# The adjacency transposed by VectorE inside the attention, with key tiles of every 13th node

## Chip, core and metric

The kernel runs on one NeuronCore of one Trainium2 chip. The metric is the device time of one execution in microseconds (us), as the median of the runs shown. One profiled execution stands beside them; its rows are used for durations. A core has five engines that run side by side: TensorE (PE; its weight loads are shown apart as PEld), VectorE (DVE), ScalarE (ACT), GpSimd (POOL) and SyncE (SP), which here issues most transfers. Sixteen DMA engines move the data between HBM and the on-chip memories.

## What is computed

Four graph layers on 3327 nodes with 128 features, each as `x = x + layer(relu(layernorm(x)))`. Only the first one is attention, and it takes most of the time. Its reshape makes 128 heads (`d`) of 8 elements (`h`) out of the projections, and the adjacency is added to the scores twice:

```python
def _L0_gnn_ref(x, spatial_encoding, edge_encoding, Wq, Wk, Wv, Wo):   # both encodings are adj
    n, d = x.shape
    h = Wq.shape[0] // d                       # 8
    scale = d ** (-0.5)
    q = (x @ Wq.T).reshape(d, n, h)
    k = (x @ Wk.T).reshape(d, n, h)
    v = (x @ Wv.T).reshape(d, n, h)
    a = jnp.einsum('dnh,dmh->dnm', q, k) * scale
    a = a + spatial_encoding + edge_encoding
    a = jax.nn.softmax(a, axis=2)
    out = jnp.einsum('dnm,dmh->dnh', a, v)
    out = out.reshape(n, h * d)
    return out @ Wo.T
```

Layers 1 and 2 are hyperbolic graph convolutions with one product `adj @ y` each. Layer 3 is a message layer with two, by rows and by columns of adj. All is in float32.

## The kernel before

The attention works on transposed scores: keys stand on the 128 partitions, queries along the free axis. So it needs adj transposed (keys by queries), and the three later layers read the same transposed copy, `adjT`, from HBM in strips.

**Head of the program.** Three stages stand ahead of the attention, each with its own pools.

- Stage a (L243 to L291): weights are transposed on TensorE, x is loaded and normalised, h is transposed (L213). Then a loop over 13 pairs of node tiles (L259) projects k, q and v (L268). q is split into a rounded half (`st_hi`, ACT, L278) and the rest (`st_lo`, DVE, L279); k is stored unsplit to `kraw_d`; squares of q and k (ACT, L281) are summed to squared norms (DVE, L283). `places` (L238) writes q and k by 1 KB runs.
- Stage b (L294 to L321): adj is read in 7 blocks of 512 rows (L302), the row maxima are taken (DVE, L305), 676 transposes on TensorE (L312) make `adjT`, where key tile tm holds the nodes tm, tm+26, tm+52 and so on: the weight operand of the transpose is `r[:m, i, tm:N:NT]`, a read with a step of 26 elements. ACT and DVE copy the results out (`evac`), SP and POOL store them (L321).
- Stage c (L328 to L377): k is read back, split into halves and reordered so that each key tile is contiguous, with reads of step 26 (L338 on ACT, L339 on DVE), and stored as `kS_d` (L341). Beside it a bound of each row's scores is worked out (norms of q and k, plus the row maximum of adj), which later stands in for the softmax's maximum, and one number, `wide`, which selects between a general path (L399, not taken with these inputs) and the fast one (L530).

**The attention** (L530 to L672) loops over 7 chunks of 476 queries, 32 groups of 4 heads and 13 pairs of key tiles: 2912 pairs. Its order is written out by hand (`manual_schedule`): one slot per head of a pair, `exps` in each slot, `scores` and `values` every second slot, `seed` and `loads` at fixed places of the four slots. For one pair u:

- `seed` (DVE, L573) copies two tiles of adj^T less the bound into two PSUM banks. Three sets of banks are used in turn, by u modulo 3.
- `scores` (PE, L579) adds the head's scores: a weight load of 64 partitions by 128 keys, `KT[b][64 * r:64 * r + 64, max(0, j - 1), q * P:(q + 1) * P]`, and 476 columns of q. Heads 1 to 3 add the difference to the head before, so a bank serves four heads in turn.
- `exps` (ACT, L591) takes exp of both banks, 952 columns. For two of three pairs the fourth head's is split in two, so that the first bank comes free earlier.
- `values` (PE, L599) multiplies by v, which stands in `VA` with a column of ones, into `po`; `store` (L611, L615) writes `po` out at the end of a group.
- `load_qk` (L488, L490, L492) brings the next group's k and q on SP's queue, `load_v` (L505) its v, `negate_q` and `spread_v` (POOL, L500, L510) prepare them, and `all_here` (POOL, L514) marks that all has come; the group's first score matmul waits for it. `load_adj` (L520, L521) brings the next chunk's adj^T.

The buffers of e stand in one ring of 16 (L464).

**After the attention** the output projection and three layers follow (L675 to L931), with `aggregate` (L747) reading strips of adjT or adj.

Of the kernel before, what the change touches and what calls it, by code (L numbers as in the profile page):

```python
# [10 lines left out]
F32 = mybir.dt.float32  # L11
# [11 lines left out]
P = 128  # L23
N = 3327
# [5 lines left out]
NQ = NT // 2  # L30
HEADS = D
# [25 lines left out]

def rows_of(t):
    return P - 1 if t == NT - 1 else P
# [15 lines left out]

@with_exitstack
def gnn_kernel(ctx: ExitStack, tc: tile.TileContext, x, adj, Wq, Wk, Wv, Wo, embed, layer,
# [8 lines left out]
    adjT = dram.tile([NT, P, NP], F32, name="adjT")  # L86
    v_d = dram.tile([NP, HD], F32, name="v_d")
    kraw_d = dram.tile([H, GP], F32, name="kraw_d")
# [3 lines left out]
    kS_d = dram.tile([2, H, HEADS, NP], F32, name="kS_d")  # L92
    oT_d = dram.tile([H + 1, GP], F32, name="oT_d")
    bound_d = dram.tile([NP], F32, name="bound_d")
    shift_d = dram.tile([HEADS, NP], F32, name="shift_d")

    rowmax = const.tile([P, NT], F32, name="rowmax")
    nc.vector.memset(rowmax, 0.0)
# [143 lines left out]

    with tc.tile_pool(name="a1", bufs=1) as a1, tc.tile_pool(name="a2", bufs=2) as a2, \  # L243
            tc.tile_pool(name="a_ps", bufs=4, space=PSUM) as a_ps:
        w_t = {"q": weight_T(a1, a_ps, Wq, "wq", "by element", HALF_SCALE),
               "k": weight_T(a1, a_ps, Wk, "wk", "by element"), "v": weight_T(a1, a_ps, Wv, "wv")}
        xs = load_x(a1)
# [9 lines left out]
        n2 = {s: a1.tile([P, NT, P], F32, name=f"n2{s}") for s in "qk"}  # L257
        v_rows = v_d.rearrange("(p t) d -> p t d", t=NT)
        for t0 in range(0, NT, 2):  # L259
            st = {s: a2.tile([P, H, 2 * P], F32 if s == "k" else F32R, name=f"st_{s}") for s in ("k", "hi", "lo")}  # L260
            sv = a2.tile([P, 2, HD], F32, name="st_v")
            for i in range(2):
                t = t0 + i
                for s in "kqv":
                    sq = a2.tile([P, HD], F32, name="sq")
                    for b in range(2):
                        ps = a_ps.tile([P, 512], F32, name="ps_m")
                        nc.tensor.matmul(ps, hT[:, t * P:(t + 1) * P], w_t[s][:, b * 512:(b + 1) * 512],  # L268
                                         start=True, stop=True)
                        if s == "v":  # L270
                            evac(sv[:, i, b * 512:(b + 1) * 512], ps)
                            continue
                        by_e = ps.rearrange("p (e i) -> p e i", e=4)
                        part = (slice(None), slice(4 * b, 4 * b + 4), slice(i * P, (i + 1) * P))
                        if s == "k":
                            evac(st["k"][part], by_e)
                        else:
                            nc.scalar.copy(st["hi"][part], by_e)  # L278
                            nc.vector.tensor_tensor(st["lo"][part], by_e, st["hi"][part].bitcast(F32),  # L279
                                                    op=ALU.subtract)  # L280
                        nc.scalar.activation(sq[:, b * 512:(b + 1) * 512], ps, AF.Square)  # L281
                    if s != "v":
                        nc.vector.tensor_reduce(n2[s][:, t, :], sq.rearrange("p (e i) -> p i e", e=H),  # L283
                                                axis=AX.X, op=ALU.add)
            nc.sync.dma_start(places(kraw_d, t0, 2, H), st["k"])
            for i, half in enumerate(("hi", "lo")):
                nc.sync.dma_start(places(qS_d, t0, 2, H, i * H * GP), st[half].bitcast(F32))
            nc.gpsimd.dma_start(v_rows[:, t0:t0 + 2], sv)
        for s in "qk":
            nc.gpsimd.dma_start(bass.AP(tensor=n2_d[s].tensor, offset=n2_d[s].offset,  # L290
                                        ap=[[NT * P, P], [1, NT * P]]), n2[s].rearrange("p t i -> p (t i)"))  # L291


    with tc.tile_pool(name="b_in", bufs=2) as b_in, tc.tile_pool(name="b_st", bufs=8) as b_st, \  # L294
            tc.tile_pool(name="b_ps", bufs=6, space=PSUM) as b_ps:
        for b in range(7):
            ts = tiles_of(b)
            nt = len(ts)
            r = b_in.tile([P, 4, N], F32, name="r")
            for i, t in enumerate(ts):  # L300
                for p0, p1 in pieces(rows_of(t)):
                    nc.sync.dma_start(r[p0:p1, i, :], adj[t * P + p0:t * P + p1, :])  # L302
            for i, t in enumerate(ts):
                m = rows_of(t)
                nc.vector.tensor_reduce(rowmax[:m, t:t + 1], r[:m, i, :], axis=AX.X, op=ALU.max)  # L305
            w = min(4 * P, N - b * 4 * P)
            for tm in range(NT):
                mp = rows_of(tm)
                ps = b_ps.tile([P, 4 * P], F32, name="ps_a")
                for i, t in enumerate(ts):  # L310
                    m = rows_of(t)
                    nc.tensor.transpose(ps[:mp, i * P:i * P + m], r[:m, i, tm:N:NT], ident[:m, :m])  # L312
                st = b_st.tile([P, 4 * P], F32, name="st_a")
                if mp < P:
                    nc.vector.memset(st, NOTHING)
                evac(st[:mp, :w], ps[:mp, :w])
                wp = w
                if b == 6:
                    nc.vector.memset(st[:mp, w:w + 1], 0.0)
                    wp += 1  # L320
                (nc.sync if tm % 2 else nc.gpsimd).dma_start(adjT[tm, :, b * 4 * P:b * 4 * P + wp], st[:, :wp])  # L321


    def head_rows(tensor):

        return bass.AP(tensor=tensor.tensor, offset=tensor.offset, ap=[[N, HEADS], [1, N]])

    with tc.tile_pool(name="c1", bufs=1) as c1, tc.tile_pool(name="c2", bufs=2) as c2, \  # L328
            tc.tile_pool(name="c_ps", bufs=2, space=PSUM) as c_ps:
        for e in range(H):  # L330
            raw = c2.tile([P, NP], F32, name="raw")
            nc.gpsimd.memset(raw[:, N:NP], 0.0)
            nc.sync.dma_start(raw[:, :N], head_rows(kraw_d[e]))
            by_tile = raw.rearrange("d (p q r) -> d r q p", q=NQ, r=2)
            hi = c2.tile([P, 2, NQ, P], F32R, name="hi")
            lo = c2.tile([P, 2, NQ, P], F32R, name="lo")
            for r in range(2):
                nc.scalar.copy(hi[:, r], by_tile[:, r])  # L338
                nc.vector.tensor_tensor(lo[:, r], by_tile[:, r], hi[:, r].bitcast(F32), op=ALU.subtract)  # L339
            for i, half in enumerate((hi, lo)):  # L340
                nc.gpsimd.dma_start(kS_d[i, e], half.bitcast(F32).rearrange("d r q p -> d (r q p)"))  # L341

        kn = c1.tile([P, NP], F32, name="kn")
        nc.sync.dma_start(kn[:, :N], head_rows(n2_d["k"]))
        km2 = c1.tile([P, 1], F32, name="km2")
        nc.vector.tensor_reduce(km2, kn[:, :N], axis=AX.X, op=ALU.max)
        qn = c1.tile([P, NP], F32, name="qn")
        nc.gpsimd.memset(qn[:, N:NP], 0.0)
        nc.sync.dma_start(qn[:, :N], head_rows(n2_d["q"]))
        nc.vector.tensor_scalar(qn, qn, km2[:, 0:1], 1e-30, op0=ALU.mult, op1=ALU.max)  # L350
        b2 = c1.tile([P, NT], F32, name="b2")
        for b in range(7):
            ts = tiles_of(b)
            ps = c_ps.tile([P, 4, P], F32, name="ps_b")
            for t in ts:
                nc.tensor.transpose(ps[:, t - 4 * b, :], qn[:, t * P:(t + 1) * P], ident)
            nc.vector.tensor_reduce(b2[:, ts[0]:ts[-1] + 1], ps[:, :len(ts), :], axis=AX.X, op=ALU.max)
        bmax = c1.tile([P, NT], F32, name="bmax")
        nc.scalar.activation(bmax, b2, AF.Sqrt)


        sh = c1.tile([P, NT], F32, name="sh")
        nc.vector.tensor_tensor(sh, bmax, rowmax, op=ALU.add)
        ps = c_ps.tile([P, P], F32, name="ps_k")
        nc.tensor.transpose(ps[:NT, :], sh, ident)
        shT = c1.tile([NT, P], F32, name="shT")
        nc.vector.tensor_copy(shT, ps[:NT, :])
        nc.sync.dma_start(bound_d.rearrange("(t p) -> t p", p=P), shT)

        fm = c1.tile([P, 1], F32, name="fm")  # L370
        nc.vector.tensor_reduce(fm, bmax, axis=AX.X, op=ALU.max)
        ps = c_ps.tile([P, P], F32, name="ps_k")
        nc.tensor.transpose(ps[:1, :], fm, ident)
        fm1 = c1.tile([1, 1], F32, name="fm1")
        nc.vector.tensor_reduce(fm1, ps[:1, :], axis=AX.X, op=ALU.max)
        wide = c1.tile([1, 1], I32, name="wide")
        nc.vector.tensor_scalar(wide, fm1, BOUND_MAX, None, op0=ALU.is_gt)  # L377
# [584 lines left out]
```

## Time and profile before

| | |
|---|---|
| median of 3 runs | 11876.81 us (11876.61 to 11879.45) |
| the profiled execution | 11879.07 us, span 11877.3 us |
| first exponential of the attention starts | 631.42 us |
| attention's last results copied out (L611) | 10761.22 us |
| ACT, L591, all exponentials | 10113.3 us busy, x13589 |
| PE, L599 and L579 | 5738.3 and 5089.5 us busy |
| DVE, L573, seeds | 3731.4 us busy, x5824 |

Times in a profile are us from the span's start unless marked ns. A group row holds line, engine, operation, result <- operands and count, then busy time and the mean of one in ns, then the engine's idle time just before those instructions and what ended it. Matmul ends are modelled, and records of one engine may overlap, so a busy share near 1 says that work follows work, not that the engine is at its peak.

### The profile page before, as it was taken

The numbers are of one execution on the slowest core, as the hardware profiler recorded it, in microseconds if no ns is written. First come the engines' busy times: TensorE is split into PE (matmuls) and PEld (weight loads), VectorE is DVE, ScalarE is ACT, GpSimd is POOL, SyncE is SP. The second block draws the span as 40 slices with busy tenths as digits, with TensorE's granted clock in tenths as the row PEclk, the third lists the DMA queues.
The fourth block names the chain that finished last, engine by engine and source line by source line (L and its number), as shares of the span: only waits on it lengthen the run. The fifth ranks groups of instructions, "written<-read, shape, count | busy, mean of one in ns | idle before, by whom it ended". The sixth has DMA issues, their size and how long they took to land.

```text
span 11877.3 us, 198965 instructions
## 1 busy us (share of the span) xinstructions
PE 11104.5 (93%) x73475; PEld 3593.7 (30%) x73475; DVE 4792.9 (40%) x7005; ACT 10457.3 (88%) x14062; POOL 1796.7 (15%) x3069
## 2 busy tenths in 40 slices
PE   6399999999999999999999999999999999996668
PEld 3322222222222222222222222222222222224334
DVE  7533333333333333333333333333333333335335
ACT  4389999999999999999999999999999999993100
POOL 0121111211121111211112111121111211110000
PEclk8699999999999999999999999999999999997789
DMA  8954444444454444544445444454444444442356
GB/s 293 367 107 79 78 82 98 84 76 82 78 101 81 77 83 76 105 77 80 80 78 104 76 84 76 81 101 79 81 76 83 99 82 79 78 85 91 137 192 239
DMA packets 532633, 1242.80 MB, mean 105 GB/s; under 512 B 148783, under 2 KB 405842, under 8 KB 509394
## 3 DMA queue, kind: packets, MB, share of 16 engines
q1 hardware_dynamic: 482013, 1051.27, 43.5%
q0 software_dynamic: 49648, 178.72, 4.6%
q8 instruction: 592, 9.70, 0.4%
q14 instruction: 380, 3.11, 0.1%
HBM read 1082.84 MB, written 146.55 MB: 104 GB/s over the span
## 4 chain that ended last, share of the span: by engine, by line
ACT 40%; PE 38%; DVE 11%; issue 9%; DMA 2%; POOL 0%; DVEq 0%; SPq 0%; POOLq 0%; ACTq 0%
ACT e L591 39%; PE S L579 16%; PE po L599 16%; DVE S L573 8%; PE pu L758 4%; PE ps_t L744 1%; PE ps_m L268 1%; DMA strip<-adjT 1%; DVE OS L611 0%; PE ps_y L703 0%; POOL adjT L321 0%; DVE s L193 0%; ACT tmp L191 0%; DMA adjT<-st_a 0%; DVE s L761 0%
## 5 line engine op out<-in xcount | busy, mean ns | idle before, releaser
L591 ACT ACTIVATE e<-S 128x952 f32<-128x952 f32 (+3 forms) x13589 | 10113.3, 915 | 14.2 <-PE S L579 7.7
L573 DVE COPY S<-a 128x476 f32<-128x476 f32 (+1 forms) x5824 | 3731.4, 655 | 6250.5 <-ACT e L591 5997.5
L599 PE MATMUL po<-e,VA 128*9 128x476 f32 (+1 forms) x46592 | 5738.3, 564 | 15.9 <-DVE OS L611 2.3
L579 PE MATMUL S<-QS,KT 64*128 64x476 f32 (+1 forms) x23296 | 5089.5, 443 | 112.9 <-DVE S L573 30.9
L579 PEld LDWEIGHTS S<-QS,KT 64*128 64x128 f32 x23296 | 2278.8, 184 | 5393.9 <-DVE S L573 2714.3
L615 POOL DMA_DIRECT2D oT_d<-OS x896 | 470.8, 531 | 6237.5 <-DVE OS L611 6157.0
L599 PEld LDWEIGHTS po<-e,VA 128*9 128x9 f32 x46592 | 691.3, 88 | 1790.4 <-issue 1691.0
L500 POOL TENSOR_SCALAR QS<-QS 32x476 fp32r<-32x476 f32 (+1 forms) x1344 | 781.9, 582 | 1034.5 <-DMA QS<-qS_d 537.7
L115 ACT COPY uT<-pu 128x494 f32<-128x494 f32 (+2 forms) x12 | 6.3, 528 | 459.2 <-PE pu L758 458.6
L758 PE MATMUL pu<-strip,y 128*128 128x494 f32 (+2 forms) x728 | 296.3, 570 | 92.8 <-DVE y L785 92.8
L758 PE MATMUL pu<-strip,h 128*128 128x494 f32 (+2 forms) x728 | 293.0, 564 | 68.9 <-DVE h L205 66.7
L510 POOL COPY VA<-VR 128x832 f32<-128x832 f32 x224 | 200.0, 893 | 962.8 <-DMA VR<-v_d 766.1
L312 PE MATMUL ps_a<-ident,r 128*128 128x128 f32 (+2 forms) x676 | 137.2, 374 | 129.2 <-DMA r<-in_adj_dram 65.3
L521 POOL TENSOR_TENSOR a<-a,shb 128x476 f32<-128x476 f32 (+1 forms) x182 | 213.1, 1203 | 239.7 <-DMA a<-adjT 239.6
L115 ACT COPY st_a<-ps_a 128x512 f32<-128x512 f32 (+3 forms) x91 | 48.5, 557 | 218.4 <-PE ps_a L312 98.1
L761 DVE TENSOR_REDUCE s<-strip 128x1 f32<-128x3327 f32 (+1 forms) x52 | 188.1, 3617 | 109.3 <-DMA strip<-adjT 63.0
L758 PEld LDWEIGHTS pu<-strip,y 128*128 128x128 f32 (+1 forms) x728 | 139.8, 192 | 248.7 <-issue 143.7
L758 PEld LDWEIGHTS pu<-strip,h 128*128 128x128 f32 (+1 forms) x728 | 138.4, 190 | 223.4 <-issue 140.7
L611 DVE COPY OS<-po 128x476 f32<-128x476 f32 (+1 forms) x224 | 145.6, 650 | 53.2 <-PE po L599 46.9
L312 PEld LDWEIGHTS ps_a<-ident,r 128*128 128x128 f32 (+2 forms) x676 | 115.8, 217 | 151.3 <-DVE st_a L119 53.5
L756 POOL DMA_DIRECT2D strip<-adjT x39 | 20.7, 532 | 793.6 <-PE pu L758 790.7
L213 PE MATMUL ps_t<-ident,h 128*128 128x128 f32 x78 | 20.3, 427 | 122.1 <-DVE h L205 108.1
(162 smaller groups left out, 1778.9 us busy)
## 6 DMA issues: line engine op xcount, KB each, us to landing
KT<-kS_d SPq DMA_DIRECT2D x1792, 208.0 KB
KT<-kS_d SPq DMA_DIRECT2D x1792, 104.0 KB
VR<-v_d SPq DMA_DIRECT2D x224, 416.0 KB
strip<-adjT POOLq DMA_DIRECT2D x39, 1663.5 KB, 8.5
strip<-adjT SPq DMA_DIRECT2D x36, 1663.5 KB
QS<-qS_d SPq DMA_DIRECT2D x3072, 14.9 KB
QS<-qS_d SPq DMA_DIRECT2D x1536, 29.8 KB
r<-in_adj_dram SPq DMA_DIRECT2D x25, 1663.5 KB
```

What stands on the lines that cost most here:

```text
L312: nc.tensor.transpose(ps[:mp, i * P:i * P + m], r[:m, i, tm:N:NT], ident[:m, :m])
L500: nc.gpsimd.tensor_scalar(QS[b][r0:r0 + 32, j + 1, :w], QS[b][r0:r0 + 32, j, :w].bitcast(F32), -1.0, 0.0, op0=ALU.mult, op1=ALU.add)
L510: nc.gpsimd.tensor_copy(VA[(c * NG + g) % 2][:, :, :, 0:H], v.rearrange("p j (t e) -> p t j e", e=H))
L521: nc.gpsimd.tensor_tensor(a[:, :w], a[:, :w], shift[:, :w], op=ALU.subtract)
L573: touch(u, [r], nc.vector.tensor_copy(bank(u, r), adj_of[c][2 * q + r][:, :w]))
L579: x = nc.tensor.matmul(bank(u, r), KT[b][64 * r:64 * r + 64, max(0, j - 1), q * P:(q + 1) * P], QS[b][64 * r:64 * r + 64, j, :w], start=Fa ...
L591: touch(u, range(a, b), nc.scalar.activation(e[:, a:b, :w], S[u % 3][:, lo + a:lo + b, :w], AF.Exp, scale=2.0))
L599: nc.tensor.matmul(po[32 * j:32 * j + H + 1, :w], VA[k % 2][:, 2 * q + r, j, :], e_of[u, j][:, at, :w], start=(q == 0 and r == 0), stop=(q ...
L611: nc.vector.tensor_copy(o[:, :w], po[:, :w])
L615: nc.gpsimd.dma_start(oT_d[:, d * N + c * CW:d * N + c * CW + w], o[32 * j:32 * j + H + 1, :w])
L758: nc.tensor.matmul(pu[c][:, :w], y[:m, t, :], s[:m, c * AW:c * AW + w], start=(t == 0), stop=(t == NT - 1))
L761: nc.vector.tensor_reduce(deg[:m, t:t + 1], s[:m], axis=AX.X, op=ALU.add)
```

## The change

- `adjT` is laid out by key in plain order (`[NP, NP]`). A key tile (r, q) holds every 13th node of one half of 1664 nodes, starting at q. So k can stay in the order of its projection: `kS_d` is written straight from stage a, split as q is, and `KT` is read by the score matmul with a step of 13 elements. The pass over `kraw_d` is gone.
- Stage b is gone. adj^T is made in 26 "squares" of 128 rows of adj, each as two halves of 1664 columns. A half is loaded so that each 32-row by 416-column part stands on a quarter of the partitions, is transposed by four DVE instructions in 32x32 blocks (`turn`), stored with runs of 512 bytes (`store`), and reduced to row maxima by four DVE instructions (`largest`). The row maxima go through HBM (`gather`, `back`) to the bound (`finish`).
- The first four squares, which the first chunk of queries needs, are made during stage a. The other 22 are made during the attention, at fixed pairs, in the chunk before the one that needs them: the load 4 pairs ahead of the first `turn`, then one DVE instruction per pair.
- Stage a projects q and k in one loop, and v in a second one. The sums of squares move from one DVE reduction to three POOL additions per tile. The bound is worked out in the middle of the v loop. x is loaded ahead of the weights.
- v of a group is loaded by two transfers with runs of 416 bytes in place of one with 832. The ring of 16 e buffers becomes one ring per head (5, 4, 3, 2). The general path is changed alike; it is not taken here.

```diff
-    adjT = dram.tile([NT, P, NP], F32, name="adjT")
+    adjT = dram.tile([NP, NP], F32, name="adjT")
+    by_key = adjT.rearrange("(r p q) n -> r q p n", r=2, q=NQ)
...
-    kS_d = dram.tile([2, H, HEADS, NP], F32, name="kS_d")
+    kS_d = dram.tile([2, H, GP], F32, name="kS_d")
...
+    class Square:
+        def load(self):
+            s, r = self.s, self.r
+            self.rows = self.pool.tile([P, 4, KW], F32, name="rows")
...
+            for i in range(4):
+                w = KW - (r == 1 and i == 3)
+                at = adj.offset + s * P * N + r * HALF + i * KW
+                nc.sync.dma_start(self.rows[32 * i:32 * i + 32, 0:whole, :w], bass.AP(
+                    tensor=adj.tensor, offset=at, ap=[[N, 32], [32 * N, whole], [1, w]]))
...
+            self.cols = self.pool.tile([P, NQ, P], F32, name="cols")
+        def turn(self, j):
+            nc.vector.transpose(self.cols[:, :, 32 * j:32 * j + 32],
+                                self.rows[:, j, :].rearrange("p (x q) -> p q x", q=NQ))
+        def store(self):
+            nc.sync.dma_start(by_key[self.r].rearrange("q p n -> p q n")[:, :, self.s * P:(self.s + 1) * P],
+                              self.cols)
+        def largest(self, rm, j):
+            nc.vector.tensor_reduce(rm[:, self.r, j:j + 1], self.rows[:, j, :], axis=AX.X, op=ALU.max)
...
+        for t0 in range(0, NT, 2):
+            for s, to in (("q", qS_d), ("k", kS_d)):
...
+                        nc.scalar.copy(st[0][part], by_e)
+                        nc.vector.tensor_tensor(st[1][part], by_e, st[0][part].bitcast(F32), op=ALU.subtract)
+                        nc.scalar.activation(sq[:, 4 * b:4 * b + 4, :], by_e, AF.Square)
+                    for m in (4, 2, 1):
+                        nc.gpsimd.tensor_tensor(n2[:, i:i + 1, :] if m == 1 else sq[:, 0:m, :],
+                                                sq[:, 0:m, :], sq[:, m:2 * m, :], op=ALU.add)
+                for half in range(2):
+                    nc.sync.dma_start(places(to, t0, 2, H, half * H * GP), st[half].bitcast(F32))
...
+            if t0 % 6 == 0 and len(bounds) < squares_of(0):
+                bounds.append(squares(a_t, len(bounds), a1))
+                bounds[-1].gather()
...
+            if t0 == 12:
+                wide = bound_scores()
...
-            v = e2.tile([P, 4, NT * H], F32, name="VR", bufs=1)
-            nc.sync.dma_start(v, bass.AP(tensor=v_d.tensor, offset=v_d.offset + 4 * g * N * H,
-                                         ap=[[NT * H, P], [N * H, 4], [1, NT * H]]))
+            for r in range(2):
+                nc.sync.dma_start(v[:, :, r * NQ * H:(r + 1) * NQ * H], bass.AP(
+                    tensor=v_d.tensor, offset=v_d.offset + (4 * g * N + r * HALF) * H,
+                    ap=[[NQ * H, P], [N * H, 4], [1, NQ * H]]))
...
-                        bank(u, r), KT[b][64 * r:64 * r + 64, max(0, j - 1), q * P:(q + 1) * P],
+                        bank(u, r), KT[b][64 * r:64 * r + 64, max(0, j - 1), q::NQ],
...
-                e = e_of[u, j] = e_e.tile([P, 2, CW], F32, name="e")
+                e = e_of[u, j] = e_e.tile([P, 2, CW], F32, name=f"e{j}", bufs=(5, 4, 3, 2)[j])
...
+            def plan_squares(c):
+                for k, s in enumerate(range(squares_of(c), squares_of(c + 1))):
+                    b = Bound(e_t, s)
+                    for r in range(2):
+                        sq, u = Square(e_t, s, r), (c * NG + 6 * k + 3 * r + 1) * NQ
+                        plan(u, sq.load)
+                        for j in range(4):
+                            plan(u + 4 + j, sq.turn, j)
+                            plan(u + 8 + j, sq.largest, b.rm, j)
+                        plan(u + 8, sq.store)
+                    plan(u + 12, b.gather)
+                    plan(u + 16, b.back)
+                    plan(u + 20, b.finish)
...
+                if at == 3 and i > 0:
+                    for f, a in behind.pop(i // 4, ()):
+                        f(*a)
...
     def strip_T(t, p0, p1):
-        return adjT[t, p0:p1, 0:N]
+        return adjT.rearrange("(p t) n -> t p n", t=NT)[t, p0:p1, 0:N]
```

## The prediction on record

> **What bounds the kernel now.** I read the slices of the page first, then its chain and groups.
>
> ```profile
> span 11877.3 us, 198965 instructions
> ...
> PE   6399999999999999999999999999999999996668
> ...
> DMA  8954444444454444544445444454444444442356
> GB/s 293 367 107 79 78 82 98 84 76 82 78 101 81 77 83 76 105 77 80 80 78 104 76 84 76 81 101 79 81 76 83 99 82 79 78 85 91 137 192 239
> ...
> ACT 40%; PE 38%; DVE 11%; issue 9%; DMA 2%; POOL 0%; DVEq 0%; SPq 0%; POOLq 0%; ACTq 0%
> ...
> L591 ACT ACTIVATE e<-S 128x952 f32<-128x952 f32 (+3 forms) x13589 | 10113.3, 915 | 14.2 <-PE S L579 7.7
> L573 DVE COPY S<-a 128x476 f32<-128x476 f32 (+1 forms) x5824 | 3731.4, 655 | 6250.5 <-ACT e L591 5997.5
> L579 PEld LDWEIGHTS S<-QS,KT 64*128 64x128 f32 x23296 | 2278.8, 184 | 5393.9 <-DVE S L573 2714.3
> ```
>
> A slice is 297 us. In the first two DMA is at 9 and 8 tenths and moves 293 and 367 GB/s while PE is at 6 and 3; then come 35 slices in which PE stays at 9 and DMA drops to 4. So the program has a head that the transfers bound, and an attention that ACT and PE bound. The windows of the head, one per stage, and one of the attention (PE, PEld, DVE, ACT, POOL busy, clock, DMA share, GB/s):
>
> ```profile
> 100.00:200.00 100.00, 84.62 (x187) 32.58 (x185) 95.35 (x94) 64.11 (x123) 3.73 (x7) 1.00 0.94 326
> 238.00:480.00 242.00, 137.23 (x676) 115.81 (x676) 149.87 (x150) 48.50 (x91) 49.21 (x92) 0.65 0.95 354
> 485.00:590.00 105.00, 6.39 (x28) 4.57 (x28) 63.29 (x30) 53.02 (x17) 9.10 (x24) 0.52 0.95 396
> 1000.00:10700.00 9700.00, 9600.47 (x66964) 2844.14 (x66963) 3702.31 (x5796) 9689.81 (x13022) 1603.01 (x2736) 1.00 0.46 84
> ```
>
> All three stages of the head keep the DMA engines at 94 or 95%: their price is their bytes. In the attention ACT is busy all the time and DMA and DVE have room. But it has a second bound, seen in a timeline of one pair:
>
> ```profile
> 5011.49 2.00 DVE L573 COPY S<-a 128x476 f32<-128x476 f32 x3 [2.10 <-ACT e L591]
> ...
> 5012.53 0.18 PEld L579 LDWEIGHTS S<-QS,KT 64*128 64x128 f32 x1 [0.80 <-DVE S L573]
> 5012.53 1.15 PE L579 MATMUL S<-QS,KT 64*128 64x476 f32 x4
> 5012.99 0.29 PEld L579 LDWEIGHTS S<-QS,KT 64*128 64x128 f32 x3 [0.28 <-DVE S L573]
> ```
>
> An exponential frees a bank, DVE seeds both banks of the pair (two copies, ending at 5012.94), the weight load of the second bank's score starts at 5012.99, its matmul ends at 5013.47, and the exponential that reads it starts at 5013.51. By the starts of single exponentials, ACT issues one every 0.843 us, but 0.945 and 0.893 us apart ahead of this one in the two kinds of pairs whose fourth exponential is split. So in two of three pairs, 1941 of 2912, ACT already waits for this chain, and any time added to a score's weight load comes out at the end 1941 times.
>
> **What goes from the head.** Stages b and c end; the old head reaches its first exponential at 631.4. The new head, built from bytes: stage a's start stays, its first projection is at 44.7, take 45 (the first half square joins DVE's work there, x comes before the weights; I set these against each other). q and k as two halves each are 4 x 13.6 = 54.5 MB, the norms 3.4 MB; at 326 GB/s, the rate of the same 1 KB runs, 178 us. ACT would need 13 x 8 x (0.59 + 0.60) = 124 us, by L278 and L281, DVE 13 x 8 x 0.68 = 71, so DMA bounds it. POOL's new additions are bounded by L521, 1.20 us for 476 columns: 896 columns by 52 tiles make 118 us, also less. Four squares of 3.4 MB each (read and written once), three of them beside the loop: 10.2 MB, 31 us. A square has one buffer each way, so SP holds back later stores until DVE has turned a half, and the next load until it is reduced. In the built program SP has the next k stores behind these. Price of a half: the transposes are in no row; below lies a plain pass, 3.62 us for 3327 columns (L761), 0.45 us for 416; above the step-26 read of stage c, 3.28 us for 1664 (L339), 0.82 us. The transpose reads with step 13, so I take 0.82; four of them and four reductions of 0.45 make 5.1 us, times 7 halves 36 us, or nothing if queued transfers cover it. v and the norms read back are 17 MB at 396 GB/s, 43 us; the bound's chain (30 us in stages b and c, from the norms' read issued at 477.6 to 508) hides behind v's stores, else it costs up to 30. Sum: 45 + 178 + 31 + 36 + 43 = 333. From the end of stage c's stores, 590, to the first exponential the old one took 41, and these steps stay: 374. The head gives 257 us.
>
> **What comes into the attention.** 22 squares bring 176 transposes and as many reductions, one per pair. DVE is idle 2.1 us before a seed that waits for ACT; an instruction of 0.45 to 0.82 us placed behind the pair's seeds ends in that gap. In every third pair the next seed follows at once, but the one that completes that pair comes 1.26 us later, which takes the delay. A late load would stop the seeds behind the transpose. But SP issues the load as soon as it is through with the group's k and v, 23 of 45 us into the group before, and the turn comes 13 us into the next one: some 30 us for 0.85 MB. In SP's queue a store of a half stands where the queue is empty: the k loads of a group are issued by 21 us after its start, and the mark that all has come is set 17.5 us before it is needed. Only at the six chunk ends is that less than 3.2 us, and no square is planned there. v's shorter runs cost DMA time in that cover. The rings of e free a buffer 4 slots before its reuse, the old ring 3. All this I cost at nothing; without cover, a late load costs what it is late, up to 44 times.
>
> **The strided weight load** is the step that decides. `KT` is now read with a step of 13 elements, 52 bytes, x23296. Stage b has weight loads of step 26, and these rows stand against contiguous ones, at full and at half clock:
>
> ```profile
> L312 PEld LDWEIGHTS ps_a<-ident,r x20: 189/200/211, 448.9 to 451.1; 128*128 128x128 f32 x20
> ...
> L699 PEld LDWEIGHTS ps_t<-ident,ot x12: 139/141/142, 10786.8 to 10788.0; 128*128 128x128 f32 x12
> ...
> L312 PEld LDWEIGHTS ps_a<-ident,r x56: 189/228/231, 238.3 to 259.4; 128*128 128x128 f32 x56
> ...
> L213 PEld LDWEIGHTS ps_t<-ident,h x11: 182/226/231, 10894.8 to 10900.0; 128*128 128x128 f32 x11
> ```
>
> At full clock (granted 1.00) the step costs 59 ns, 200 against 141; at half clock (0.51 and 0.50) nothing, 228 against 226. So the read has a pace of its own, which shows only where the load is faster than it. The score's load takes 184 ns already, contiguous and at full clock, near the strided 200. Bounds of what is added: nothing; 59 ns if the difference carries over; and, the farthest row, DVE's 1.97 ns a column (L339), 252 ns for 128, against 107 ns between the starts of two consecutive loads of a score block: 145 ns. A gain is excluded, since the same words are read. I take 7 ns, from the row that is nearest in kind, the pace in a run: at full clock 20 strided loads take 2.38 us (from 448.89), 0.119 each, and 12 contiguous ones 1.34 us (from 10786.82), 0.112 each. That is 1941 x 0.007 = 14 us.
>
> The Trainium skill, "SBUF — State Buffer", section "Door 1: The DMA port swizzle", speaks against the change: on-chip reads keep full rate only with two hits per 16-byte line, so float32 may step by 4 elements at most, and this steps by 13. It gives no price for weights; by it the 59 ns would be the term, and the sum 101 us worse. The equal rows at half clock speak for a limit that the score load barely meets.
>
> **Sum.** 11879.1 - 257 + 14 = 11636 against the profiled execution; that one lies 2.3 us above the median, so **11634**.
>
> **Rivals.**
> - The load pays the full 59 ns: 1941 x 0.059 = 115 in place of 14, so 11735. For it: the row at full clock. Against: the score load is slower already.
> - The load goes at DVE's strided pace: 1941 x 0.145 = 281 in place of 14, 11901, **slower than before**. It decides from 257 / 1941 = 0.132 us upward. Against: a strided load of 128 columns takes 200 ns in all.
> - The head doesn't empty as told: SP's waits last twice as long, v hides nothing, and 70 more remain: 36 + 30 + 70 = 136, 11770. For it: one queue, one buffer.
> - The squares don't fit beside the seeds: 44 halves with 5 us of late data each, 220 us, 11854, about no change. Against: 30 us of lead.
>
> **How the numbers follow.** Forecast 0.62; full 59 ns 0.16; DVE's pace 0.08; slow head 0.08; late squares 0.06. Some 0.2%, 24 us, is what a measurement tells from no change: the first, second and fourth case are faster, 0.86, and some of the fifth, 0.02, of whose chance 0.04 is same; the third is slower, 0.08. Range: the forecast's low end has no SP waits (36) and no strided price (14) and half of v in the loop's gaps (21), 11563; the high end takes in the second and fourth case, 11775, leaving 0.14 out.
>
> **What would show it.** First exponential near 374 us; the exponentials' stretch still 10130 us long, with L573's waits on ACT as before; the score's weight load at 184 to 200 ns; transposes at 0.45 to 0.82 us without DMA as a seed's releaser. I am wrong if the weight load is above 240 ns, if the first exponential comes after 450, or if ACT's idle time before its exponentials passes 100 us with DVE behind it.

## The result, and the profile after

The changed kernel takes 12054.58 us (median of 4 runs, 12051.49 to 12062.81) against 11877.78 (4 runs beside it): a ratio of 1.015, 95% interval 1.0132 to 1.0167. It is 177 us slower, where 243 us faster were forecast. The page of its profiled execution (12062.81 us) says where to look first; these lines answer to those shown of before, with span, slices, the chain by engine, and three groups:

```profile
span 12060.9 us, 195358 instructions
...
PE   5899999999999999999999999999999999996668
...
DMA  9655545555455444554545555455544544442456
GB/s 285 128 86 85 90 74 111 88 83 89 77 108 89 86 79 76 109 90 84 87 79 105 90 87 84 82 104 90 88 76 79 97 80 77 78 78 84 147 186 238
...
PE 87%; DMA 6%; DVE 3%; ACT 2%; SPq 1%; issue 1%; POOL 1%; DVEq 0%; ACTq 0%; POOLq 0%
...
L630 ACT ACTIVATE e<-S 128x952 f32<-128x952 f32 (+3 forms) x13589 | 10359.3, 857 | 188.4 <-PE S L618 173.7
L612 DVE COPY S<-a 128x476 f32<-128x476 f32 (+1 forms) x5824 | 3739.8, 654 | 6233.6 <-ACT e L630 5976.6
...
L618 PEld LDWEIGHTS S<-QS,KT 64*128 64x128 f32 x23296 | 3744.8, 339 | 4804.7 <-ACT e L630 2344.0
```

The head shows at once: the second slice has PE at 8 and DMA down at 6, so the attention begins within it. But the chain has changed hands. Before, ACT carried 40% of the span and PE 38%; now PE carries 87% and ACT 2%. ACT was idle 14.2 us ahead of its exponentials and is now idle 188.4, waiting for scores. The weight load of the scores went from 184 to 339 ns mean.

Two rows by line give the ends of both stages. The columns are shortest, median and longest in ns, then the first and last start:

```profile
L630 ACT ACTIVATE e<-S x13589: 557/963/1014, 389.6 to 10936.7; 128x952 f32<-128x952 f32 x123, 128x476 f32<-128x476 f32 x49, 128x944 f32<-128x944 f32 x20, 128x472 f32<-128x472 f32 x8
```

```profile
L618 PEld LDWEIGHTS S<-QS,KT x23296: 324/328/358, 386.2 to 10935.6; 64*128 64x128 f32 x200
```

The first exponential starts at 389.6 instead of 631.4: the head gave back 242 us. The stretch of the exponentials grew from 10127 us (631.4 to 10758.3) to 10547: 420 us lost. The tail behind the last exponential is 1124 us against 1119. So 242 won and 425 lost make the 183 us between the two profiled spans, and all but 5 us of the loss is in the attention. ACT's idle time of 188.4 us does not show all of it: its records overlap, and their busy time grew by 246 us although the mean of one fell from 915 to 857 ns. The load's row has no fast case at all: its shortest is 324 ns, where before the shortest was 182 and the median 183.

The longer weight load is a first suspect for the loss. A second stands in the list of waits (total us, times, longest):

```profile
DVE b L308 <- DMA four<-rowmax_d: 144.4, 22, 8.3
```

22 is the number of squares in the attention. L308 is the first line of `finish`, which reduces the four partial row maxima of a square, and `four` is the small read of them from HBM that `back` (L304) issues. (From 1000 to 10800 us alone the wait is 129.5 us, 20 times; the first expectation below goes by that.) One of these in a timeline (start, us, engine, line; in brackets the idle time before and what ended it):

```profile
653.88 0.66 SPq L529 DMA_DIRECT2D QS<-qS_d  x2
654.64 0.94 SPq L543 DMA_DIRECT2D VR<-v_d  x2
655.63 0.50 SPq L304 DMA_DIRECT2D four<-rowmax_d  x1
...
658.46 0.16 DVE L308 TENSOR_REDUCE b<-four 128x1 f32<-128x4 f32 x1 [8.29 <-DMA four<-rowmax_d]
...
659.04 1.96 DVE L612 COPY S<-a 128x476 f32<-128x476 f32 x3
...
661.34 1.82 ACT L630 ACTIVATE e<-S 128x952 f32<-128x952 f32 x2 [6.85 <-PE S L618]
```

On SP's queue the read of `four` stands behind the next group's q, k and v. It is issued at 655.63, when the last of these is through, and lands some 2.8 us later. DVE had reached `finish` long before and stood there for 8.29 us, with the next pair's seeds behind it in its queue. They start at 659.04, and ACT, which needs the scores on top of them, was idle 6.85 us.

So there were two suspects: **A**, the stepped weight load; **B**, the late `four` under `finish`. A rival to both is that the cost is the transposes in DVE's queue or the new DMA traffic. Within A it is open whether the load costs by its place in the chain from seed to exponential (latency) or by PE's total work (pace).

### The profile page after: what moved, and what is told of

Its sections match the earlier page's. It is cut to its first block, busy times and chain, and to the rows that moved or that the text cites. A ratio compares the mean times of both kernels' runs of the same rounds, so it can differ in the third digit from the quotient of the medians.

```text
span 12060.9 us, 195358 instructions
## 1 busy us (share of the span) xinstructions
PE 11421.9 (95%) x72798; PEld 4955.8 (41%) x72798; DVE 4807.2 (40%) x7304; ACT 10618.0 (88%) x13981; POOL 1881.1 (16%) x3162
## 4 chain that ended last, share of the span: by engine, by line
PE 87%; DMA 6%; DVE 3%; ACT 2%; SPq 1%; issue 1%; POOL 1%; DVEq 0%; ACTq 0%; POOLq 0%
PE po L638 42%; PE S L618 40%; PE pu L822 4%; DMA QS<-qS_d 2%; DMA KT<-kS_d 1%; ACT e L630 1%; DMA strip<-adjT 1%; PE ps_t L808 1%; DMA four<-rowmax_d 1%; POOL sq L368 0%; PE ps_y L767 0%; DVE s L202 0%; ACT tmp L200 0%; DMA v_d<-st_v 0%; PE ps_t L348 0%
## 5 line engine op out<-in xcount | busy, mean ns | idle before, releaser
L630 ACT ACTIVATE e<-S 128x952 f32<-128x952 f32 (+3 forms) x13589 | 10359.3, 857 | 188.4 <-PE S L618 173.7
L618 PEld LDWEIGHTS S<-QS,KT 64*128 64x128 f32 x23296 | 3744.8, 339 | 4804.7 <-ACT e L630 2344.0
L618 PE MATMUL S<-QS,KT 64*128 64x476 f32 (+1 forms) x23296 | 5495.3, 523 | 120.4 <-DVE S L612 116.1
L279 DVE STREAM_TRANSPOSE cols<-rows 128x416 f32<-128x416 f32 x208 | 187.9, 912 | 15.9 <-DMA rows<-in_adj_dram 15.9
```

The source lines that it names most:

```text
L279: nc.vector.transpose(self.cols[:, :, 32 * j:32 * j + 32], self.rows[:, j, :].rearrange("p (x q) -> p q x", q=NQ))
L618: x = nc.tensor.matmul(bank(u, r), KT[b][64 * r:64 * r + 64, max(0, j - 1), q::NQ], QS[b][64 * r:64 * r + 64, j, :w], start=False, stop=Tr ...
L630: touch(u, range(a, b), nc.scalar.activation(e[:, a:b, :w], S[u % 3][:, lo + a:lo + b, :w], AF.Exp, scale=2.0))
```

## The experiments

**Each suspect alone, and both.** In the first run only `finish` is later:

```diff
-                    plan(u + 20, b.finish)
+                    plan(u + 24, b.finish)
```

> The kernel after, with the last step of a square of the bound, `finish`, planned 4 slots later (24 pairs behind the square's start instead of 20, some 14 us). Theory: the small read `four` stands in SP's queue behind the next group's k, q and v, so that `finish` holds DVE's queue up to 7.6 us, 22 times; with 14 us more it has landed. The 129.5 us that DVE waits for `four` fall below 10, and the time falls by 140 to 165, from 12054.6 to 11890-11915. Rival: what the squares cost is their transposes of 0.92 us in DVE's queue and the DMA traffic, and the wait only takes time in which DVE would have idled: 12035-12055.

Measured: 11900.75 us, 154 less than the changed kernel and 1.0021 of before (1.0011 to 1.003). The 26 instructions of L308 show no idle time before them any more. B is worth about what its stalls add up to: 154 us, or 7 for each of the 22, where the waits came to 144.4. The page shows what is left, and a window of the attention (PE, PEld, DVE, ACT, POOL busy, clock, DMA share, GB/s) how full PE is:

```profile
PE 92%; DVE 2%; issue 1%; DMA 1%; ACT 0%; SPq 0%; POOL 0%; POOLq 0%; ACTq 0%; DVEq 0%
```

```profile
1000.00:10700.00 9700.00, 9700.00 (x65231) 4136.89 (x65224) 3828.28 (x6025) 9665.59 (x12684) 1567.29 (x2692) 1.00 0.52 88
```

PE's records leave no gap in 9700 us; ACT's leave 34.

The second run reads the weights contiguously. The scores are then of other keys than their tile of adj^T, here and wherever the step is changed below without a reordering of k, so these runs give a time and not a usable kernel:

```diff
-                        bank(u, r), KT[b][64 * r:64 * r + 64, max(0, j - 1), q::NQ],
+                        bank(u, r), KT[b][64 * r:64 * r + 64, max(0, j - 1), q * P:(q + 1) * P],
```

> The kernel after, with the score's weights read contiguously (128 neighbouring keys in place of every 13th; the scores are then of other keys than the tile of adj^T that they are added to). Theory: the strided read is 0.145 us a load and the load stands in the chain from seed to exponential; the load falls from 328 to 183 ns and the time by 240 to 270, to 11785-11815. Rival: the chain has room that the trace does not show, or the longer loads come from the added traffic rather than the step: the load stays above 250 ns or the time falls by less than 100, to above 11955.

Measured: 11781.86 us, 273 less, 0.9923 of before (0.9906 to 0.994); 3 us below the expected range. The load is back at 185 ns mean, and the wait for `four` is still there:

```profile
L618 PEld LDWEIGHTS S<-QS,KT 64*128 64x128 f32 x23296 | 2286.2, 185 | 5522.6 <-DVE S L612 2804.9
```

```profile
DVE b L308 <- DMA four<-rowmax_d: 154.9, 22, 9.3
```

Both edits together:

> Both edits in one (late `finish` and contiguous weights; the scores are of other keys than their tile of adj^T). Theory: the two losses are at different places and add up: 12054.6 less 250 less 155, 11635-11670, which is what the forecast gave. Rival: with one gone the other is hidden or shows a third cost (transposes, late loads of a square): 11700-11800.

Measured: 11615.66 us, 0.9784 of before (0.9767 to 0.98): 439 less than the changed kernel, where the single edits gave 154 and 273, and 19 us below the expected range. The 12 us beyond the sum fit the waits for `four`: with contiguous weights DVE reaches `finish` sooner and waits 154.9 us in all, 10 more than in the changed kernel.

```profile
ACT 80%; PE 9%; issue 5%; DVE 3%; DMA 1%; POOL 1%; SPq 0%; DVEq 0%; POOLq 0%; ACTq 0%
...
L630 ACT ACTIVATE e<-S 128x952 f32<-128x952 f32 (+3 forms) x13589 | 10106.9, 914 | 8.0 <-PE S L618 7.1
```

The chain is ACT's again, with 8.0 us of idle time. The exponentials run from 378.3 to 10492.6, 10114 us against 10127 before the change. So with A and B gone, all that the squares bring into the attention, transposes, loads, stores and more packets, costs nothing there.

**The step without the rest of the change.** The kernel before, with the score's weights read by `q::NQ` in place of `q * P:(q + 1) * P` (L579), nothing else changed:

> The kernel before, with nothing changed but the read of the score's weights: a step of 13 (the scores are of other keys than their tile of adj^T). Theory: the load goes from 183 to 328 ns without any of the new traffic, and the time rises by 240 to 285, to 12117-12162, by the chain in two of three pairs (1941 x 0.145 = 281 at most). Rival: only together with the squares' work does the load cost this much: below 11950.

Measured: 12174.9 us, 1.0253 of before (1.0236 to 1.027), 299 more. So A needs neither squares nor their traffic. But it is also a miss: 299 is above 281, the most that 1941 waits of 0.145 us can give. Either more pairs wait than those, or something beside the chain's latency pays. The timeline shows a candidate, first in the kernel before, then in this one:

```profile
5010.98 0.30 PEld L579 LDWEIGHTS S<-QS,KT 64*128 64x128 f32 x4 [0.80 <-ACT e L591]
5010.99 0.70 PE L579 MATMUL S<-QS,KT 64*128 64x476 f32 x4
...
5011.61 0.12 PEld L599 LDWEIGHTS po<-e,VA 128*9 128x9 f32 x8 [0.33 <-issue]
```

```profile
5011.62 0.58 PEld L579 LDWEIGHTS S<-QS,KT 64*128 64x128 f32 x4 [0.80 <-ACT e L591]
5011.62 0.88 PE L579 MATMUL S<-QS,KT 64*128 64x476 f32 x4
...
5012.43 0.12 PEld L599 LDWEIGHTS po<-e,VA 128*9 128x9 f32 x8 [0.22 <-issue]
...
5013.34 0.77 PEld L579 LDWEIGHTS S<-QS,KT 64*128 64x128 f32 x4 [0.80 <-DVE S L573]
```

A block of four score loads and matmuls holds PE 0.63 us until the value loads begin (5010.98 to 5011.61), and with the step 0.81 (5011.62 to 5012.43). The eight values behind it take 0.91 to the next scores (5012.43 to 5013.34). Two such rounds make a pair: about 3.08 us contiguous, 3.44 with the step. The 2912 pairs come every 3.48 us before (10127 us in all) and every 3.58 here (627.4 to 11051.3). PE had 0.4 us of every pair to catch up after a wait for a seed; with the step it has 0.1.

**Latency or pace.** On the kernel with the late `finish`, the step in the first head's loads alone (e5), and in all but these (e6). In short:

```diff
+ e5:  q::NQ if j == 0, else q * P:(q + 1) * P
+ e6:  q::NQ if j > 0,  else q * P:(q + 1) * P
```

> From here on the base has the late `finish`: 11900.8 with the step of 13 in all score weights, 11615.7 with contiguous ones. Here the step is only in the loads of the pair's first head (j = 0); the other three are contiguous, with scores of other keys. Theory L (latency): the 0.146 us from a seed's end to the end of its matmul delay the first exponential of two pairs in three and nothing else costs, so nearly the whole loss is here: 11870-11905. Rival T (pace of PE): a block of four score loads and the eight value loads behind it take 1.54 us contiguous and 1.72 with the step, two such rounds per pair are 3.07 and 3.45 us, against 3.37 that ACT needs, so the loss comes from all four heads together; with one head stepped a quarter to a half of it: 11660-11750.

> The reverse: contiguous weights for the first head (scores of other keys), the step of 13 for heads 1 to 3. Theory L: these loads lie in cover, 11615-11640. Rival T: three quarters to half of the loss, 11750-11850.

Measured: 11802.95 us with the step in the first head, 11665.99 with it in the other three. Over 11615.7 that is 187 and 50 of the 285 that the step costs in all four heads; 48 come only from both together. Neither expectation holds. Two thirds of the price come with the first head: these loads are a quarter of all, and they are the ones behind a seed. That speaks for latency. The other three quarters of the loads cost 50 alone. The last 48 fit a late block that meets a PE without room to catch up, but no run varies that room by itself.

**Which steps pay.** Same base, with a start kept inside the tile:

```diff
-                        KT[b][64 * r:64 * r + 64, max(0, j - 1), q::NQ]
+ e7:                    KT[b][64 * r:64 * r + 64, max(0, j - 1), min(q * P, HALF - 255):][:, 0:255:2]
+ e8:                    KT[b][64 * r:64 * r + 64, max(0, j - 1), min(q * P, HALF - 509):][:, 0:509:4]
+ e11:                   KT[b][64 * r:64 * r + 64, max(0, j - 1), min(q * P, HALF - 382):][:, 0:382:3]
```

> Late `finish`, and the score weights read with a step of 2 (8 bytes; the scores are of other keys than their tile of adj^T). Theory: the read pays per 16 bytes fetched, and two words of each 16 bytes are still used: load 183 to 190 ns, 11610-11630. Rival: the price rises with the step from the first: load 200 to 250 ns, 11680-11780. The Trainium skill, 'Advanced Engine Details and Errata', section 'SBUF Cachelines', states lines of 16 bytes and that two hits in a line absorb the access latency; it speaks for the theory.

> Late `finish`, and the score weights read with a step of 4 (16 bytes, one word of each; other keys). Theory: full price as with 13, load 320 to 330 ns, 11885-11915. Rival, price by the step: load 230 to 290 ns, 11720-11830; a rival that a step up to 4 is free: 183 ns, 11610-11630.

> Late `finish`, score weights read with a step of 3 (12 bytes; the scores are of other keys). 128 words then lie in 96 lines of 16 bytes, against 32, 64 and 128 with steps of 1, 2 and 4 (183, 191 and 308 ns). Theory of a price per line above 64: load about 250 ns, time between 11640 and 11740. Rival, a word alone in its line makes the whole load slow: 300 ns or more, 11780-11810; rival, only a step of 16 bytes or more pays: 195 ns, 11615-11630.

The rows of the load in these runs, steps 2, 3 and 4:

```profile
L618 PEld LDWEIGHTS S<-QS,KT x23296: 189/191/333, 380.3 to 10501.0; 64*128 64x128 f32 x200
```

```profile
L618 PEld LDWEIGHTS S<-QS,KT x23296: 247/249/328, 381.7 to 10562.4; 64*128 64x128 f32 x200
```

```profile
L618 PEld LDWEIGHTS S<-QS,KT x23296: 304/308/335, 376.7 to 10676.9; 64*128 64x128 f32 x200
```

| step | lines of 16 bytes for 128 words | load, median ns | time, us | over step 1 |
|---|---|---|---|---|
| 1 | 32 | 183 | 11615.7 | |
| 2 | 64 | 191 | 11620.8 | 5 |
| 3 | 96 | 249 | 11682.6 | 67 |
| 4 | 128 | 308 | 11799.6 | 184 |
| 13 | 128 | 328 | 11900.8 | 285 |

Up to 64 lines the load hardly changes; from there 32 lines more cost 58 and 59 ns, 1.8 ns a line. The times expected for steps 2 and 3 (a price per line) hold. The one for 4 misses by 85 us, since its load stays 20 ns under that of 13; the time is in the range of the rival, a price by the step, though the load of 308 ns is not. Why 13 costs those 20 ns more with as many lines stays open, and no step between 4 and 13 was run, so that the line of 16 bytes is what fits the five figures and not the only reading of them.

The time grows faster than the load: 58 ns cost 62 us, the next 59 ns 117, the last 20 ns 101. PE's round goes with it. A block of four score loads that waits for no seed takes 0.63, 0.69 and 0.77 us to the values with steps 2, 3 and 4, the last one here:

```profile
5002.79 0.54 PEld L618 LDWEIGHTS S<-QS,KT 64*128 64x128 f32 x4 [0.80 <-ACT e L630]
...
5003.56 0.12 PEld L638 LDWEIGHTS po<-e,VA 128*9 128x9 f32 x8 [0.23 <-issue]
```

With 0.91 for the values, two rounds leave some 0.4, 0.3 and 0.2 us of a pair (3.47, 3.50 and 3.54 us by the stretch of the exponentials), and 0.1 with step 13. So the price per ns rises as the room in PE's round goes; that the room is the reason is argued, not shown.

**Is it SP's order?** The changed kernel with only the read moved, ahead of the next group's loads:

```diff
-                    plan(u + 16, b.back)
+                    plan(u + 13, b.back)
```

> The changed kernel, step of 13 and `finish` where it was, with only the small read `four` issued 3 pairs earlier, ahead of the next group's k, q and v in SP's queue. Theory: the read was late because of what stood before it in the queue; ahead of it it lands in a few us and the waits go, as with a late `finish`: 11890-11920, DVE's wait for `four` below 10 us. Rival: the read itself or the stores of the row maxima that it waits for are slow: the wait stays above 60 us and the time above 11960.

Measured: 11902.28 us, 1.0022 of before (1.0012 to 1.0031), as with the late `finish`, and L308 has no idle time before it. The square of the timeline above now has its read issued at 624.46 in place of 655.63, 31 us earlier for three pairs of the plan (some 11 us), since 29 us of loads stood between:

```profile
L308 DVE TENSOR_REDUCE b<-four 128x1 f32<-128x4 f32 x26 | 3.7, 149 | 0.0
```

```profile
624.46 0.38 SPq L304 DMA_DIRECT2D four<-rowmax_d  x1
...
644.52 0.15 DVE L308 TENSOR_REDUCE b<-four 128x1 f32<-128x4 f32 x1
```

The read is quick by itself, some 2.8 us in the changed kernel; its place in the queue made it late.

**A kernel that beats both.** Late `finish`, and k reordered in the head as in stage c before, now with tiles of every 13th node:

```diff
+            raw = c2.tile([P, NP], F32, name="raw")
...
+            nc.sync.dma_start(raw[:, :N], head_rows(kraw_d[e]))
+            by_tile = raw.rearrange("d (r p q) -> d r q p", q=NQ, r=2)
...
-                        bank(u, r), KT[b][64 * r:64 * r + 64, max(0, j - 1), q::NQ],
+                        bank(u, r), KT[b][64 * r:64 * r + 64, max(0, j - 1), q * P:(q + 1) * P],
```

> A whole kernel that computes everything: the changed one with the late `finish`, with k put into key-tile order once in the head again (projected unsplit, read back, split and reordered, 27 MB more than in the changed kernel), so that the score weights are contiguous. Theory: 11616 as with contiguous weights, plus 27.3 MB at 354 GB/s, 77 us, plus up to 30 for a stage with its own start and end: 11690-11725, faster than before by 150 to 190. Rival: the pass can't run beside the v projection and its strided reads on ACT and DVE bound it: 11750 or more.

Measured: 11683.68 us (5 runs, 11682.07 to 11687.83), 0.9838 of before (0.9824 to 0.9851): 193 us faster, and 6 us below the expected range. The exponentials start at 448.4, 70 us later than at 378.3 with contiguous weights and no reordering, and run 10115 us:

```profile
L659 ACT ACTIVATE e<-S x13589: 558/1008/1101, 448.4 to 10562.9; 128x952 f32<-128x952 f32 x123, 128x476 f32<-128x476 f32 x49, 128x944 f32<-128x944 f32 x20, 128x472 f32<-128x472 f32 x8
```

This kernel computes everything. So adj^T made beside the attention, with q and k ahead of v, is worth 193 us even with k reordered; leaving k unordered saves 70 in the head and costs 285 in the loop.

## Why the prediction was wrong, step by step

- **What bounds the kernel**: right as far as it went (ACT, and behind it the chain seed, weight load, matmul, exponential). It missed that PE's round of scores and values, 3.08 of 3.48 us, was a further bound close by, though the rows of the round stood in the timeline of before.
- **The head**: right in mechanism, 242 us for 257. The first exponential came at 389.6 for 374. The sum took 326 GB/s for the q and k loop; the window below has the DMA engines full at 287. SP's waits for a square are there, too: before 400 us its queue waits 52.5 us for transposed halves, 7 times, where the sum had 36 us. How much of that the queued transfers cover stays open.

```profile
100.00:200.00 100.00, 53.87 (x88) 20.86 (x86) 46.53 (x76) 44.38 (x83) 62.95 (x84) 0.80 1.02 287
```

```profile
SPq L283 <- DVE cols L279: 52.5, 7, 12.6
```

- **The squares at nothing**: "All this I cost at nothing" failed, by 154 us, for an instruction that the step never named. It followed the loads, the stores and the transposes of a square, and these are free: a transpose takes 917 ns for the 0.82 us taken, a reduction 576 for 0.45, and still the stretch without A and B is 10114 us. It did not follow the four row maxima, the smallest transfer of all. That SP "is through with the group's k and v, 23 of 45 us into the group before" was used for the loads; the same number says that a read planned at pair 3 of a group is issued only then, and `finish` stands at pair 7. The rival of late squares had the engine and the kind (a DMA behind SP's queue under a DVE instruction), but named another transfer and gave 220 us.

```profile
L279 DVE STREAM_TRANSPOSE cols<-rows x208: 795/917/941, 28.0 to 8735.5; 128x416 f32<-128x416 f32 x104
```

- **The strided weight load**: "I take 7 ns" failed; it is 145. That is the far end of the bounds to the ns, DVE's strided pace carried over to 128 columns, but by chance: that bound took a load of 252 ns, and less 107 ns "between the starts of two consecutive loads". The load lasts 328, and the 107 ns lie between two pairs of loads, as the two of a pair start 3 ns apart. The row nearest in kind, PE's own loads with a step of 26, misled: there strided and contiguous loads came 0.119 and 0.112 us apart. The equal durations at half clock and the total of 200 ns were read as a pace that the score load barely meets; but nothing in those rows showed that 200 ns is all that a stepped load of another operand takes. The factor 1941 was a fair size (299 and 285 us measured, for 281), but partly by luck: the step in the first head alone, whose loads are those of the chain, costs 187 us, which is 0.145 us 1290 times. The rest came with the other heads, which the prediction did not count and whose price is best explained by PE's pace.
- **The Trainium skill**, "SBUF — State Buffer", section "Door 1: The DMA port swizzle", was weighed against the change and set aside; its direction was right. Its lines of 16 bytes, with full rate at two hits in each, fit these runs: a step of 2 costs 8 ns. Its figure of a free step of 4 in float32 does not hold for these loads, which pay 125 ns with it; the measurement decides.
- **Rivals**: the one at DVE's pace put the time at 11901, slower than before. The changed kernel without the stall under `finish`, which no case had, takes 11900.8. That the two agree is luck in part, as 98 of the 285 us are not the first head's alone. With neither loss it takes 11615.7, near the forecast of 11634.
- **What was to show it**: two of three alarms rang, the load above 240 ns (328) and ACT's idle time above 100 us (188.4).

## What to carry to other kernels

Before an operand of a loop's matmuls is read with a step, count how many 16-byte lines it touches, and price the load at the far bound if it stands in the chain that the loop waits for; check as well how much of the loop's period the engine has left. When work is moved behind a hand-ordered loop, follow each of its instructions down to the smallest read: where it stands in its queue, and which in-order engine waits on it. Here a read of 2 KB, 22 times, cost 154 us, and issuing it three pairs earlier gave them back.

## What the runs showed of the hardware

- A weight load of 64 x 128 float32 words takes 183, 191, 249, 308 and 328 ns with steps of 1, 2, 3, 4 and 13 words: 8 ns more at two words per 16 bytes, then 1.8 ns for each line more up to a step of 4.
- The price of a longer load rises as it grows: over 23296 loads, the 58 ns from step 2 to 3 cost 62 us, the 20 ns from 4 to 13 cost 101.
- VectorE's transpose of 128 x 416 words, read with a step of 13, takes 917 ns, 2.2 ns a column; 176 of them in the loop cost it nothing (10114 us in the run without the two losses, 10127 in the kernel before).
